# Two graph attention layers from neighbor lists: a reworked prelude, the 20-node block in another PSUM tile, and layer 1 with each product ahead of the next sums

## The chip, the cores and the metric

The kernel runs on one core of one Trainium2 chip. The metric is the device time of one execution in microseconds (us), from the start to the end of the program; the kernel before has a median of 1781.02 us. A core has five engines with instruction queues of their own: PE (TensorE, matrix products into PSUM), DVE (VectorE), ACT (ScalarE), POOL (GpSimd) and SP (SyncE, which here only issues DMAs). ACT and POOL issue DMAs too; all gathers and scatters by index are issued by POOL.

## The reference

Two layers on a graph of N = 2708 nodes with features of D = 1024, in f32. `adj` is a dense 2708 x 2708 matrix of 0 and 1 with about 17 ones in a row.

```python
# layer 0
f = x @ Wf + bf;  g = x @ Wg + bg
e = relu(f @ g.T)
att = softmax(where(adj > 0, e, NEG), axis=1)
x = layernorm(x + att @ (x @ W + bW))
# layer 1
h = x @ W1;  f1 = h @ a1;  f2 = h @ a2
e = leaky_relu(f1 + f2.T, 0.2)
att = softmax(where(adj > 0, e, NEG), axis=1)
x = layernorm(x + relu(att @ h))
```

Each node attends to its neighbors alone, so the kernel never forms an N x N product. With M = Wf Wg^T the score of nodes i and j in layer 0 is x_i M x_j plus terms of the biases. In layer 1, f1 = x (W1 a1) and f2 = x (W1 a2), so the two vectors u1 = W1 a1 and u2 = W1 a2 are enough for the scores. In both layers the neighbors' rows are summed first and multiplied with the weight after that: (att @ x) W.

## The kernel before

**Queues.** `pe`, `dve`, `act`, `pool` and `sp` are wrappers (class `InOrder`, L61) that keep what is issued through them in the order of the program text; the profile shows all of it at L71. What is written with `nc.vector` or `nc.gpsimd` instead may be moved by the scheduler of the framework.

**Prelude (L249 to L511).** For each of 22 blocks of 128 rows of `adj` (the last has 20 rows, the "20-node block") `lists(b)` (L402) loads the block into one of three `adj` tiles through SP, ACT casts it and counts its ones (`Relu` with a sum), POOL multiplies it by `iota`, which falls from 8192 along a row (L409), so that a one becomes a number that tells its column, and DVE takes the eight largest of each of 20 segments (`MAX8`, L412) and from these the 40 largest of the row (L414 to L418), and then the number of neighbors and its class (L420 to L425). Three blocks later `keep_lists` (L427) has ACT turn the result into indices and write them to DRAM (`LD`). Beside that runs the generator `weights()` (L292), one step of it for each block: it loads rows of Wg, Wf and W1 (through ACT's queue), turns them on PE (`turned`, L281: eight 128 x 128 transposes for a tile of 128 rows), and computes M in 16 products (`m_product`), two bias rows (`c_product`), and u1 and u2 (`u_product`). The result of a product leaves PSUM for SBUF on ACT one step later (the list `late`, emptied by `flush`). `row_parts` (L252) splits a bias row into three bf16 rows on POOL: three casts, three small DMA issues and two subtractions. Many constants are filled by POOL at the head of the program (L150 to L233).

When all blocks are done, each node gets its place by the number of its neighbors (L451 to L502, the "rank stage"): the results `ids`, the node at each place, and `idq`, where its list lies. Places are cut into 22 new blocks of 128 (block 0 has 20 nodes in 32 places), and these into 85 groups of 32. A group of class t has `TILES` = t tiles, and a tile is one gather of 128 rows: four neighbors for each of the group's 32 nodes. Block 0 has 3 tiles, blocks 1 and 21 have 15, blocks 19 and 20 have 16, blocks 2 to 18 have 20: 405 gathers in each layer.

**Layer 0 (L757 to L985)** takes the blocks as units in the order 1, 0, 2, ..., 21. A unit's rows x are gathered (`load_x`), turned, and multiplied by M (`f_product`), the result is replicated four times (`Fr`, on ACT); POOL gathers the neighbors' rows into a ring of 20 slots; DVE forms one dot product for each tile (`dots`) and the softmax weights (`soft`); PE sums the weighted rows (`Layer.sums`, L693: first the row sums `rs`, then one half of a tile after the other into the PSUM tile `po`), turns the sum y and multiplies it by W, held in `Wt`; `close` (L828) adds x and norms. The result goes to X1S and, with f2 = x u2 in a further column, is scattered by POOL to the table T1. The PSUM pool `ps_m` has two tiles `pm`, `ps_t` has two tiles `pt`, `ps_s` one tile `po`. L858 to L906 are the start: unit 1's product is made in two halves (L877), then the 20-node block's (`f_small`, L799, with `split_product`, L558, which spreads its 8 steps over four groups of 32 columns and lets a second matmul with `rep` add the four parts), then unit 2's (`f_product(2)`); ACT issues the load of W into `Wt` (4.19 MB) at L900, behind the copies that precede it in the program.

**Layer 1 (L988 to L1111)** takes the blocks in the order 0 to 21 with a ring of 32 slots (`ring` and `more`). The rows of T1 are gathered; DVE forms the scores from the f2 column (`scores1`); in step k PE forms the sums of block k, and then the product of block k-1 with W1 (`M` holds W1 by then), and then turns y of block k (L1079 to L1089). `close1` (L1027) takes relu, the residual and the norm of the block before that, and its scatter to the output is issued inside a later block's sums (the hook 6 at L1079). After the last step come the last turn, the last product (in two PSUM tiles) and the closing of the last two blocks. A slot of the ring is free, and the gather for it is issued, where the sums have used it (L725 to L727).

## Time and profile before

| | us |
|---|---|
| median of 3 runs (1780.73 to 1785.28) | 1781.02 |
| the profiled execution's own time | 1778.93 |
| its span, first to last instruction | 1777.1 |
| of it: prelude and rank stage, 0 to 218 | 218 |
| layer 0, 218 to the first gather of layer 1 | 939 |
| layer 1, 1157 to the end | 620 |

The same three stretches by engine (busy us):

| stretch | PE | DVE | ACT | POOL | DMA engines' mean share |
|---|---|---|---|---|---|
| 0 to 218 | 171.1 | 171.8 | 109.4 | 162.6 | 54% |
| 218 to 1157 | 877.6 | 773.8 | 445.5 | 589.1 | 72% |
| 1157 to 1777 | 524.4 | 225.9 | 81.5 | 430.8 | 90% |

The profile is one execution. "Busy" is the time in which an engine works on an instruction; what an engine waits for is told by the waits (waiter, releaser, total, times, longest) and by the timelines (start, duration, engine, line, operation, output and inputs, and in brackets the idle time before it and what ended it). A row "x8" stands for eight like instructions in a row with their total. In the page's slices, the span is cut in 40 equal parts, here of 44.4 us, and a digit is the busy share in tenths. The load of W by ACT is a DMA: its engine is busy for the issue alone, and the transfer shows in the DMA share.

### The profile page before, as it was taken

How to read it: one execution, taken by the hardware profiler on the slowest of the kernel's cores; microseconds unless marked ns; L12 is line 12 of the kernel's file. 1: busy time of each engine (PE TensorE's matmuls, PEld its weight loads, DVE VectorE, ACT ScalarE, POOL GpSimd, SP SyncE). 2: the span in 40 equal slices, each digit the busy share in tenths (PEclk: the TensorE clock that was granted, in tenths of full speed). 3: DMA queues.
4: the chain of work that ended last, by engine and by line, in shares of the span. 5: the costliest groups of instructions: out<-in, count | busy, mean ns of one | idle time of the engine just before them, and what ended most of it. 6: DMA issues, size and time to landing. Idle time of an engine off the chain costs nothing. (4 is left out here: it accounts for less than half of the span.)

```text
span 1777.1 us, 22911 instructions
## 1 busy us (share of the span) xinstructions
PE 1573.1 (89%) x7313; PEld 667.6 (38%) x7313; DVE 1171.4 (66%) x3539; ACT 636.4 (36%) x861; POOL 1182.5 (67%) x1191
## 2 busy tenths in 40 slices
PE   4999479899999999999999999637989988989996
PEld 2444234344444444444444444213333333333342
DVE  5879855888888888988888887513342433424442
ACT  4544454444444455555555544101111111111111
POOL 7878476467666666666666663177777777777740
PEclk9999779999999999999999999959989999999998
DMA  7646168568777777777777777299999999999960
GB/s 283 237 169 238 40 233 301 208 224 296 282 285 274 264 250 255 280 284 287 279 291 283 268 281 281 103 358 346 363 386 392 392 364 394 384 392 388 366 259 37
DMA packets 149982, 501.86 MB, mean 282 GB/s; under 512 B 32565, under 2 KB 32597, under 8 KB 147144
## 3 DMA queue, kind: packets, MB, share of 16 engines
q0 software_dynamic: 132032, 427.36, 64.8%
q1 hardware_dynamic: 10202, 55.72, 8.3%
q10 hardware_dynamic: 7618, 17.23, 2.7%
q8 instruction: 59, 0.97, 0.2%
q14 instruction: 71, 0.58, 0.1%
HBM read 509.64 MB, written 33.75 MB: 306 GB/s over the span
## 5 line engine op out<-in xcount | busy, mean ns | idle before, releaser
L71 POOL DMA_INDIRECT ring<-in_x_dram,SL x405 | 432.0, 1067 | 256.2 <-issue 89.0
L71 DVE SCALAR_TENSOR_TENSOR j<-ring,Fr 128x1024 bf16<-128x1024 f32 x402 | 494.9, 1231 | 77.0 <-DMA ring<-in_x_dram,SL 49.8
L71 ACT COPY Fr<-pm 32x1024 f32<-32x1024 f32 (+2 forms) x353 | 340.5, 965 | 20.0 <-PE pm L71 15.3
L71 PE MATMUL po<-ring,st 128*32 128x512 f32 x2660 | 338.6, 614 | 0.1
L71 POOL DMA_INDIRECT ring<-T,SL x260 | 259.6, 998 | 83.8 <-issue 58.0
L71 PE MATMUL pm<-M,xT 128*128 128x512 f32 (+1 forms) x704 | 309.7, 617 | 0.4 <-ACT xT L71 0.4
L71 PE MATMUL pm<-Wt,xT 128*128 128x512 f32 (+1 forms) x704 | 303.5, 599 | 0.0
L71 PE MATMUL pm<-M,yT 128*128 128x512 f32 (+1 forms) x704 | 298.5, 595 | 0.3 <-ACT yT L71 0.3
L71 ACT ACTIVATE scores<-scores 128x24 f32<-128x24 f32 (+5 forms) x44 | 9.8, 222 | 640.7 <-DVE scores L71 640.7
L71 PEld LDWEIGHTS pm<-M,yT 128*128 128x128 f32 (+1 forms) x704 | 127.2, 186 | 170.2 <-issue 169.7
L71 PEld LDWEIGHTS pm<-M,xT 128*128 128x128 f32 (+1 forms) x704 | 127.0, 190 | 170.6 <-issue 169.9
L71 PEld LDWEIGHTS pm<-Wt,xT 128*128 128x128 f32 (+1 forms) x704 | 125.0, 186 | 151.8 <-issue 151.4
L71 POOL DMA_INDIRECT more<-T,SL x145 | 144.1, 994 | 44.0 <-issue 32.8
L71 PEld LDWEIGHTS po<-ring,st 128*32 128x32 f32 x2660 | 102.5, 114 | 183.9 <-issue 180.0
L71 DVE TENSOR_SCALAR scores<-ring,f1q 128x2 f32<-128x2 f32 (+5 forms) x98 | 21.8, 245 | 211.3 <-DMA ring<-T,SL 209.6
L409 POOL TENSOR_TENSOR adj<-adj,iota 128x2708 f32<-128x2708 f32 (+3 forms) x23 | 130.5, 5684 | 24.9 <-ACT adj L71 24.8
L71 ACT ACTIVATE y<-po,ri 128x512 f32<-128x512 f32 (+1 forms) x88 | 55.8, 683 | 232.5 <-PE po L71 214.6
L412 DVE MAX8 cand<-adj 128x8 f32<-128x136 f32 (+2 forms) x440 | 97.2, 284 | 37.4 <-POOL adj L409 37.4
L71 PE MATMUL pm<-halfT,WfT 128*128 128x512 f32 x256 | 113.9, 600 | 1.1 <-ACT WfT L71 1.1
L71 POOL DMA_INDIRECT SL<-LD,idq x85 | 85.5, 1006 | 25.8 <-issue 20.9
L71 PE MATMUL pt<-rs,stack 128*32 128x1 f32 x680 | 14.1, 179 | 98.0 <-DVE rs L71 53.4
L71 PE MATMUL po<-more,st 128*32 128x512 f32 x580 | 94.2, 651 | 0.0
(198 smaller groups left out, 1416.9 us busy)
## 6 DMA issues: line engine op xcount, KB each, us to landing
adj<-in_adj_dram SPq DMA_DIRECT2D x21, 1354.0 KB, 5.8
X1S<-z SPq DMA_DIRECT2D x20, 512.0 KB, 6.4
ring<-in_x_dram,SL POOLq DMA_INDIRECT x405, 6.2
u1b<-X1S SPq DMA_DIRECT2D x11, 512.0 KB
rb<-X1S SPq DMA_DIRECT2D x10, 512.0 KB, 7.3
ring<-T,SL POOLq DMA_INDIRECT x260, 7.3
rows<-in_L_gnn_Wg_dram ACTq DMA_DIRECT2D x8, 512.0 KB, 4.5
rows<-in_L_gnn_Wf_dram ACTq DMA_DIRECT2D x8, 512.0 KB, 3.6
```

Of the source, the lines that this page charges most:

```text
L71: made = self.tc.keep_in_program_order(op(*args, **kwargs))
L409: nc.gpsimd.tensor_tensor(k[:n, cut], k[:n, cut], iota[:n, cut], op=ALU.mult)
L412: nc.vector.max(cand[:n, s, :], k[:n, s * SEG:min((s + 1) * SEG, N)])
```

## The change

Three parts of the program change.

*Prelude.* u1 and u2 are no longer made on PE. The eight turned tiles of W1, `u_product` and the loads for them go; `W1` is loaded whole into `Wt` by SP at the start of layer 0, `a1` and `a2` are broadcast to all partitions by two DMAs of POOL in the middle of the prelude (into `u1b` and `u2b`), 16 dot products on DVE (`u_dots`) give the two columns, and `u_spread` brings them back into `u1b` and `u2b` as rows on all partitions: 16 matmuls and four ACT copies. There are four `adj` tiles instead of three. The first block is loaded, cast and multiplied in two parts, the second block is multiplied in two. The 20-node block of `adj` comes in the middle of the order instead of last, as four quarters of its columns on four groups of partitions (`tail`), so that a segment's `MAX8` serves four. The constants are filled by `pool` in four batches after the third to the sixth block. `weights()` yields a cost at each step (1 for a turned tile, 6 for a product), and the loop takes steps up to 6.5 units a block. POOL does one multiply (`same` by `early`) of the rank stage, whose tiles come from a pool of their own, `places`.

*Start of layer 0.* The 20-node block's product uses the sums' tile `po` (`ps_s`) for its first part and no longer waits for one of the two `pm`; unit 2 is turned earlier; `f_product(2)` comes directly after that, and the 20-node block's second part after that. The issue of the load of W now stands behind `u_spread`'s copies.

*Layer 1.* The blocks are ordered by the number of their tiles (0, 1, 21, 19, 20, 2, ..., 18). In step k the sums of a block are followed by the turn and the product of the same block, and by its `close1`; its scatter is issued inside the next block's sums.

The diff, cut to what matters (a removed line of one of the functions printed above is left out in places, and so is the rank stage but for its multiply):

```diff
+        def constants():
+            pool.memset(quad, 0.0)
+            for q in range(Q):
+                rows = slice(32 * q, 32 * q + 32)
+                pool.tensor_copy(stack[rows], ident[rows, rows])
+                pool.memset(quad[rows, q:q + 1], 1.0)
...
+                pool.memset(t, v)
+            yield
...
-        with tc.tile_pool(name="adjp", bufs=3) as adjp, tc.tile_pool(name="cands", bufs=2) as cands, \
+        with tc.tile_pool(name="adjp", bufs=4) as adjp, tc.tile_pool(name="cands", bufs=2) as cands, \
...
-                def u_product(h, wT):
...
                 WgT[1] = half_tile()
                 for k in range(KC):
-                    flush()
                     turned(WfT[:, :, k * P:(k + 1) * P])
+                    yield 1
...
+                        row_parts(brow[:, half], b3[:, half])
+                    yield 6
...
-                flush()
+                    yield 6
                 c_product(1)
-                yield
-                flush()
...
+                yield 6
...
+                if b == NB - 1:
+                    k = tail.bitcast(F32)
+                    act.activation(k, tail, AF.Relu, accum_out=tails)
+                    cand4 = cands.tile([P, NSEG // 4, 8], F32, name="cand4", bufs=1)
+                    for c in range(4):
+                        rows = slice(32 * c, 32 * c + 32)
+                        pool.tensor_tensor(k[rows], k[rows], iota[rows, c * quarter:(c + 1) * quarter],
+                                                op=ALU.mult)
+                    for s in range(NSEG // 4):
+                        nc.vector.max(cand4[:, s, :], k[:, s * SEG:min((s + 1) * SEG, quarter)])
+                    for c in range(4):
+                        rows = slice(32 * c, 32 * c + n)
+                        nc.vector.tensor_copy(cand[:n, c * NSEG // 4:(c + 1) * NSEG // 4, :], cand4[rows])
+                        pool.tensor_copy(tail4[:n, c:c + 1], tails[rows])
...
+                else:
+                    t = adjp.tile([P, N], I32, name="adj")
+                    k = t.bitcast(F32)
+                    cuts = [slice(0, 10 * SEG), slice(10 * SEG, N)]
+                    for i, cut in enumerate(cuts if b == 0 else [slice(0, N)]):
+                        sp.dma_start(t[:n, cut], adj[b * P:b * P + n, cut])
+                    for i, cut in enumerate(cuts if b == 0 else [slice(0, N)]):
+                        act.activation(k[:n, cut], t[:n, cut], AF.Relu,
+                                       accum_out=tot[:n, b:b + 1] if i == 0 else tot2[:n])
+                        if b == 0 and i == 0:
+                            load_weights(3)
+                    for cut in cuts if b < 2 else [slice(0, N)]:
+                        pool.tensor_tensor(k[:n, cut], k[:n, cut], iota[:n, cut], op=ALU.mult)
...
+            blocks = list(range(NB - 1))
+            blocks.insert(NB // 2, NB - 1)
+            steps, done, some = weights(), 0, constants()
+            act.activation(tot2, ones, AF.Relu)
+            for i, b in enumerate(blocks):
                 lists(b)
-                if b > 2:
-                    keep_lists(b - 3)
-                if b == 4:
...
+                if 2 <= i < 6:
+                    next(some, None)
+                if i == 6:
+                    pool.memset(tail, 0)
+                    for c in range(4):
+                        pool.dma_start(tail[32 * c:32 * c + few, :], adj[N - few:, c * quarter:(c + 1) * quarter])
+                if i == 8:
                     fill_highs()
-                if b > 0:
-                    next(steps, None)
-            for b in range(NB - 3, NB):
+                if i in (13, 15):
+                    u, a = (u1b, a1) if i == 13 else (u2b, a2)
+                    pool.dma_start(u, a.rearrange("d o -> (d o)").partition_broadcast(P))
+                flush()
+                while done < (2 * i if i < 3 else 6.5 * i - 13.5):
+                    cost = next(steps, None)
+                    if cost is None:
+                        break
+                    done += cost
+            for b in blocks[-3:]:
                 keep_lists(b)
             for _ in steps:
...
+            nc.gpsimd.tensor_tensor(same, same, early, op=ALU.mult)
...
+    def split_product(xT, w, parts, row=None, pm=None):
...
+        pm = ps_m.tile([P, H, 512], F32, name="pm") if pm is None else pm
...
+        yield
...
+        sp.dma_start(Wt, W1.rearrange("(k p) d -> p k d", p=P))
...
-        def f_small():
-            pm = whole(split_product(xTs.pop(0), M, yp.tile([P, D], F32, name="y"), 0))
...
+        def u_dots(k0, k1):
+            for k in range(k0, k1):
+                for i, u in enumerate((u1b, u2b)):
+                    dot(Wt[:, k, :], u, P, ucols[:, i, k:k + 1])
+        def u_spread(i):
+            u = (u1b, u2b)[i]
+            pts = []
+            for k0 in range(0, KC, 4):
+                pt = ps_t.tile([P, 4, P], F32, name="pt")
+                for k in range(4):
+                    pe.matmul(pt[:, k, :], ucols[:, i, k0 + k:k0 + k + 1].to_broadcast([P, P]), ident,
+                              start=True, stop=True)
+                pts.append(pt)
+            yield
+            for k0, pt in zip(range(0, KC, 4), pts):
+                act.copy(u[:, k0 * P:(k0 + 4) * P], pt.rearrange("p k i -> p (k i)"))
...
         load_lists(0)
+        u_dots(0, 2)
         q_dot(1)
...
+        u_dots(2, KC)
+        for _ in spread0:
+            pass
+        xTs[2] = tp.tile([P, KC, P], F32, name="xT")
+        turn2 = turn(xb[2], nrows[2], xTs[2])
+        next(turn2)
+        small_f = split_product(xTs.pop(0), M, yp.tile([P, D], F32, name="y"), 0,
+                                ps_s.tile([P, H, 512], F32, name="po"))
+        next(small_f)
...
+            for _ in turn2:
+                pass
+        next(small_f)
...
-        f_small()
-        x_turn(2)
...
+        spreads = [u_spread(0), u_spread(1)]
+        next(spreads[0])
         f_product(2)
+        for _ in spreads[0]:
+            pass
+        next(spreads[1])
+        Fr[0, 0] = zs[:, :D]
+        act.copy(Fr[0, 0], flat(whole(small_f)))
+        for _ in spreads[1]:
+            pass
         spread2 = q_spread(2)
         next(spread2)
         act.dma_start(Wt, W.rearrange("(k p) d -> p k d", p=P))
...
-        first_gathers(5, NSL0)
+        for g in range(5, max(g for _, g, _ in lay.order[:lay.count]) + 1, 4):
+            first_gathers(g, g + 4)
...
+        order1 = sorted(range(NB), key=lambda b: (sum(TILES[g] for g in groups[b]), b))
+        units = cut(R1, Q, order1)
...
-        waiting = []
         for k, u in enumerate(units):
...
-                count_over()
-            lay.sums(u, po, {6: [lambda s=closing: [None for _ in s]]}, y[b])
-            closing = iter(())
-            if back is not None:
-                if back > 0:
-                    prod[back] = product(P, yTs.pop(back)[0], M)
-                else:
-                    prod[back] = whole(split_product(yTs.pop(back)[0], M, z1[1]))
+            y = yp.tile([P, D], F32, name="y1")
+            lay.sums(u, po, {6: [lambda s=closing: [None for _ in s]]}, y)
             yT = tp.tile([P, KC, P], F32, name="yT")
-            steps = turn(y.pop(b), nrows[b], yT, halves=True)
-            next(steps)
-            yTs[b] = yT, steps
-            if waiting:
-                closing = close1(waiting.pop())
-                next(closing)
-            if back is not None:
-                waiting.append(back)
-            if nxt is not None:
-                scores1(nxt)
+            for _ in turn(y, nrows[b], yT, halves=True):
+                pass
+            if k + 1 == NB:
+                prod = two_products(P, yT, M)
+            elif b > 0:
+                prod = product(P, yT, M)
+            else:
+                prod = whole(split_product(yT, M, z1[1]))
             for i in (2 * k, 2 * k + 1):
                 if i < NB:
                     mark_over(i)
+            if k == NB // 2 + 1:
+                count_over()
+            if k + 1 < NB:
+                scores1(units[k + 1])
+            closing = close1(b, prod)
+            if k + 1 < NB:
+                next(closing)
             if k + 2 == NB:
                 unfit = nc.values_load(flag[0:1, 0:1])
         for _ in closing:
             pass
-        b = NB - 1
-        for _ in yTs[b][1]:
-            pass
-        prod[b] = two_products(P, yTs.pop(b)[0], M)
-        for b in waiting + [b]:
-            for _ in close1(b):
-                pass
     return unfit
```

## The prediction

> **What bounds the kernel now.** I read the page first (engines, then slices), then the waits of the first 206 us, the engines' timelines at the start of layer 0, and POOL's and PE's timelines at the end of layer 1. The page:
>
> ```profile
> span 1777.1 us, 22911 instructions
> PE 1573.1 (89%) x7313; PEld 667.6 (38%) x7313; DVE 1171.4 (66%) x3539; ACT 636.4 (36%) x861; POOL 1182.5 (67%) x1191
> ...
> PE   4999479899999999999999999637989988989996
> ...
> DMA  7646168568777777777777777299999999999960
> ```
>
> No engine is the limit throughout. Slices 1 to 5 (to 220 us) are the prelude. Slices 6 to 25 are layer 0, where PE stands at 9 and DMA at 7; its loop, which the change leaves alone from the third unit on, is PE's. Slices 26 to 38 are layer 1 with DMA at 9. In the prelude the waits say more than the busy shares:
>
> ```profile
> DVE cand L412 <- POOL adj L409: 37.4, 13, 12.8
> ACT M L71 <- PE pm L71: 33.1, 9, 5.0
> ACT adj L71 <- DMA adj<-in_adj_dram: 25.6, 7, 7.5
> POOL adj L409 <- ACT adj L71: 24.8, 11, 7.2
> ```
>
> (Columns: waiter, releaser, us in total, times, longest.) DVE's sort of 22 adjacency blocks sets the end, and it starves: POOL's product is late because ACT's relu is late, because ACT queues behind copies of matmuls, or because the three `adj` tiles are all held. DVE begins at 13.8, ends the lists at 206.0, and the indices `ids` are complete at 217.9. At layer 1's end POOL's timeline (start, us, what, idle before) reads
>
> ```profile
> 1707.46 0.99 POOL L71 DMA_INDIRECT ring<-T,SL  x1 [0.30 <-issue]
> 1708.75 0.99 POOL L71 DMA_INDIRECT ring<-T,SL  x1 [0.30 <-issue]
> 1710.05 0.99 POOL L71 DMA_INDIRECT more<-T,SL  x1 [0.30 <-issue]
> ```
>
> one gather each 1.295 us without a gap since 1157.4: 404 steps x 1.295 = 523, 18 scatters 24, memsets and hiccups 6, sum 553 = 1710.05 - 1157.4. POOL's issue rate bounds layer 1; the transfers keep pace. Then PE:
>
> ```profile
> 1724.36 1.04 PE L71 MATMUL pt<-ident,y 128*128 128x128 f32 x8
> 1725.69 0.31 PE L71 MATMUL pt<-rs,stack 128*32 128x1 f32 x16 [0.29 <-ACT yT L71]
> ...
> 1732.82 14.00 PE L71 MATMUL pm<-M,yT 128*128 128x512 f32 x32
> 1746.66 1.04 PE L71 MATMUL pt<-ident,y 128*128 128x128 f32 x8
> 1747.99 14.00 PE L71 MATMUL pm<-M,yT 128*128 128x512 f32 x32 [0.29 <-ACT yT L71]
> ```
>
> The last sums (1725.8) are followed by the product of the block before (1732.8) and only then by their own (1748.0): 14 us of the tail belong to an earlier block.
>
> **What the skill says.** Trainium skill, "DMA: Bandwidth & Descriptors", section "Issuing engines are not separate DMA queues": DMAs from ACT, SP and POOL run on the same 16 engines and interleave. The trace agrees: from 276 to 280 us the load of W took 53% of the engines and the gathers 50%. "TensorE: Matmul & The Clock Gate", section "What's actually happening": the clock halves after about 3.4 us of idle. Here an idle of 2.69 us at 1655.5 was followed by about 3 us of matmuls at 1.07 us, one of 2.34 at 1629.1 was not.
>
> **Part 1, the prelude.** Removed from PE: 8 turned W1 tiles at 1.1 us of transposes (8.8) and two `u_product`s at 7.1 (14.2), 23 us. PE then has 16 tiles (18), 16 M products at 7.1 (114) and two c products (14): 146 us, spread at 6.5 units a block, 7.7 us, beside DVE's 7.3 to 8.2. Four `adj` tiles take away the 25.6 us wait: a tile's turn is load 5.8, relu 2.7, POOL 5.9, sort 7.5, sum 22, which three tiles give every 7.3 us and four every 5.5.
>
> What is next late is POOL. The order of the built kernel puts both `row_parts` of bW (6.8 us each: three casts of 0.6, three issues of 0.5, two subtractions of 1.15, gaps) right before the third and fourth block's products, and the constants (about 1 us a batch) before the next ones. POOL, from the halved first block (load of half about 5.0, relu 1.4, product from 6.7): blocks 0, 1 done at 12.7 and 18.9, block 2 at 31.6, block 3 at 45.6, block 4 at 52.8, then 6 to 7 a block, tail at 104, block 13 at 130.3 (a `row_parts` more), block 20 at 173. DVE against this, with 4.1 us for the 20 MAX8 and 4.0 for the chain, 0.22 for each pair member where two blocks are interleaved: from 9.7, blocks 0 and 1 done at 27, block 2 31.6 to 39.9, blocks 3 and 4 45.6 to 62.2, block 7 started at 78.6, block 10 done 109.5, the tail (5 MAX8, 4 copies, chain: 5.9) 115.4, block 14 144, block 17 167, block 20 191.7. The two early stalls (about 5 and 6 us) stay; later DVE is never without work. ACT's lists for block i-3 stand before its copies, so relu(i) comes about 8 us after DVE ends block i-4, 8 us before POOL's result is needed: hidden. End of the lists 191.7 instead of 206.0, **-14.3**. The rank stage loses one DVE multiply (0.64) to POOL: **-0.5**. `c3`'s last parts on POOL end near 201, `ids` at 203, so the first gather isn't held (2 us of cover).
>
> W1's load on SP waits for the last c product, about 167; 4.19 MB in 13 to 14 us (the load of W took 14) is there by 182. Four dots at 1.28 (5.1 us) fit before the first `xb` lands (5.55 us idle at 217.9), twelve (15.3) in the 14.64 us that DVE idles at 230 to 244.9: about 0.5 late, 0. Without that cover they cost 20. The two broadcasts of a1, a2 are one POOL issue each, in the sum above.
>
> **Part 2, the start of layer 0,** on the clock of before (all of it shifts by 14.8). Now:
>
> ```profile
> 263.81 1.04 PE L71 MATMUL pt<-ident,xb 128*128 128x128 f32 x8
> ...
> 280.13 0.31 PE L71 MATMUL pt<-rs,stack 128*32 128x1 f32 x16
> ...
> 293.91 7.13 PE L71 MATMUL pm<-Wt,xT 128*128 128x512 f32 x16
> ```
>
> The small block waited 9.19 us for a `pm` tile (to 254.0). In `po` it runs at 245.8 to 252; the f product takes the freed `pm` at 255.4 (the ACT copies are 1.1 later for xT) and ends at 270.3, then 8 u matmuls (1.1) and the replication (2.0): first sums at 273.6, against 280.1; DVE is ready at 272.9. That is -6.5. But ACT's issue of W now stands behind copies of `u2b`, which stand behind the replication: 275.7 instead of 264.9. In before it was alone for most of its 14 us; now gathers for the third unit start at 276 and take half: 4.19 MB at 205 GB/s is 20.4 us, landing at 298.3. PE wants it at 287.6 (293.9 - 6.3). The product goes to 298.4, and third sums from 327.1 to about 329: **+2**. Bounds: W in time, DVE then sets the third sums at 321.3, -5.8; slow clock after the 11 us idle, +4. I take +2, since the shared rate is measured.
>
> **Part 3, layer 1.** Units ordered by tiles (3, 15, 15, 16, 16, then 17 of 20); each product follows its own turn. PE's round of 20 tiles: row sums 0.4, sums 8.85, wait for y 0.86 and transposes 1.23 (as at 1125), wait 0.29, product 13.86: 25.5. POOL's round: 20 gathers and a scatter, 21 x 1.295 = 27.2. So POOL stays the bound. At the start PE lags by up to 6.5 us on units 2 to 4 (sums at 1214, 1238, 1262), but slot reuse asks for less: POOL reaches tile 81 at 1268, freed at 1263. Scatters fall 6 gathers after the sums start and their block is normed 7.2 us after it, POOL reaches them 13.7 after: hidden. DVE's order (scores, then close, then the next reciprocal) leaves the reciprocal 3 us before it is used.
>
> End: 20 scatters instead of 18 stand before the last gather, +2.6: issued at 1712.7; row sums ready 10.9 later, as before (1710.05 to 1721.0): 1723.6; sums of 20 tiles to 1732.9; turn 2.4; product 14.0, 1749.3; and 15.1 from the last product to the end (1762.0 to 1777.1): 1764.4. **-12.7**. Bounds: -6 (PE late by 6) and -14 (no second scatter).
>
> **Sum.** -14.3 - 0.5 + 2 - 12.7 = -25.5, on a span of 1777.1: 1751.6. That execution took 1778.93, 1.8 around its span, and the runs' median 1781.02 is 2.1 above it. Carrying both: 1755.5.
>
> **Rivals.** (A) The sum above, 1755.5, own range 1747 to 1764: 0.60. (B) The prelude gains little: POOL, whose 160 us of work stay, slips a few us in each of the 22 products, or ACT's lists tie relu to DVE; lists end near 203, gain 3: 1768. For it: DVE already ran at 19.3 of 20 from 140 to 200. Against: 37.4 us of starvation lie ahead of that. 0.18. (C) Everything fits: the row parts wait elsewhere, DVE runs through (9.7 + 21 x 7.5 + 5.5 = 173, but POOL's 173 + 8 forbids less than 181), -25; W in time, -6; tail -14: 1738. 0.14. (D) Slower: PE becomes layer 1's bound. Its gap of 1.15 a unit was seen only in layer 0 and singly; over 17 units at 27.2, a round of 29.0 eats the 25.5 and 5 more. At 29.5 (a gap of 5 us, clock down after it) it is +39: 1794. Against: 1746.66 to 1747.99 shows the turn-to-product wait at 0.29. 0.08. That the dots' move saves nothing is in B: PE was not DVE's only cover.
>
> **Chances.** 0.3% (5.3 us) is what a measurement can tell from no change: faster below 1775.7, B's upper fringe (0.03) lies at it. Faster 0.60 + 0.15 + 0.14 = 0.89; same 0.04; slower 0.07. Range 1740 to 1770: A, nearly all of B, half of C.
>
> **What would show it.** DVE's first MAX8 near 10, lists' end near 192 with idles of about 5 before blocks 2 and 3; no wait of ACT on `adj` loads of several us; the first sums (unit 1) at about 259 and the first Wt product at about 283.5, after an idle of PE near 11; POOL at 1.295 a gather through layer 1; last product directly behind the last turn, and 52 us from the last gather's issue to the end, where it was 67. It is wrong if POOL has gaps in layer 1 (D), or if DVE waits past block 4 (B).

## The result and the profile after

The changed kernel takes 1771.74 us (median of 6 runs, 1765.66 to 1779.03) beside 1781.88 us (6 runs, 1780.73 to 1785.39) for the kernel before: ratio 0.9936, interval 0.9917 to 0.9955. It is faster by 10.1 us. 25.5 were forecast, and 1771.74 lies 1.7 above the range. The profiled execution took 1770.84 us with a span of 1769.1, against 1778.93 and 1777.1: 8.0 us of span to account for. Read by marks in both traces (the end of the last list, taken at the first instruction of the rank stage; the first gather of layer 0; the third unit's sums; the first and the last gather of layer 1; the end):

| stretch | before | after | difference | predicted |
|---|---|---|---|---|
| prelude, to the end of the lists | 206.1 | 202.9 | -3.2 | -14.3 |
| rank stage, to the first gather | 12.7 | 15.1 | +2.4 | -0.5 |
| start of layer 0, to the third sums | 108.2 | 110.8 | +2.6 | +2.0 |
| layer 0's loop | 830.3 | 829.3 | -1.0 | 0 |
| layer 1, first to last gather issued | 552.7 | 561.0 | +8.3 | +2.6 |
| tail, to the end | 67.0 | 49.9 | -17.1 | -15.3 |
| sum | 1777.1 | 1769.1 | -8.0 | -25.5 |

So the end of layer 1 came about as foretold and the prelude did not. The page of the kernel after, engines and slices:

```profile
span 1769.1 us, 22760 instructions
PE 1563.6 (88%) x7217; PEld 660.3 (37%) x7217; DVE 1198.7 (68%) x3559; ACT 629.2 (36%) x840; POOL 1188.8 (67%) x1210
...
PE   4799289899999999999999999839998988889896
...
DMA  7655268567777777777777787289999999999990
```

PE's 23 us of products for u1 and u2 are gone from its first slices, yet the prelude still fills five of them. The waits of its first 206 us (waiter, releaser, us in total, times, longest):

```profile
ACT M L71 <- PE pm L71: 22.8, 8, 5.4
...
DVE cand L423 <- POOL adj L71: 16.1, 6, 8.6
DVE cand L423 <- POOL quad L71: 12.7, 1, 12.7
ACT adj L71 <- DMA adj<-in_adj_dram: 10.3, 10, 2.7
...
POOL adj L71 <- ACT adj L71: 6.7, 4, 2.7
```

ACT's wait for `adj` loads fell from 25.6 to 10.3 and POOL's for ACT from 24.8 to 6.7, as was predicted. But DVE still waits 16.1 + 12.7 = 28.8 us for POOL (37.4 before), and 12.7 of that in one piece, ahead of block 2. POOL's timeline there (start, us, what, idle before and what ended it):

```profile
23.74 0.60 POOL L265 CAST part<-u1b 1x512 bf16<-1x512 f32 x1 [4.98 <-DMA u1b<-in_L_gnn_bW_dram]
...
31.52 0.60 POOL L265 CAST part<-rest 1x512 bf16<-1x512 f32 x1 [2.27 <-DMA rows<-part]
32.41 0.53 POOL L266 DMA_DIRECT2D rows<-part  x1 [0.29 <-POOL part L265]
32.96 5.93 POOL L71 TENSOR_TENSOR adj<-adj,iota 128x2708 f32<-128x2708 f32 x1
38.81 0.12 POOL L71 MEMSET quad<- 128x4 f32 x1
```

The row parts of bW stand ahead of block 2's product, as predicted; that POOL would wait 4.98 us for bW itself and 2.27 us for a row's DMA was not predicted. Block 2 is ready at 38.9 instead of 31.6.

The start of layer 0:

```profile
265.10 0.38 PE L71 MATMUL pm<-rows,ones 3*128 3x512 bf16 x1
265.42 7.13 PE L71 MATMUL pm<-M,xT 128*128 128x512 f32 x16
...
279.79 9.63 PE L71 MATMUL po<-ring,st 128*32 128x512 f32 x60 [0.22 <-issue]
...
295.68 4.56 PE L71 MATMUL pm<-Wt,xT 128*128 128x512 f32 x10
```

The 9.19 us wait for a `pm` tile is gone, but the first sums stand 61.1 us after the first gather, where they stood 61.3, and they take 9.63 us. In the kernel before they took 7.07:

```profile
280.58 7.07 PE L71 MATMUL po<-ring,st 128*32 128x512 f32 x60
```

The product with `Wt` begins without a wait for the load of W. And the end of layer 1, POOL and PE:

```profile
1717.87 0.99 POOL L71 DMA_INDIRECT ring<-T,SL  x1 [0.30 <-issue]
1719.17 0.99 POOL L71 DMA_INDIRECT more<-T,SL  x1 [0.30 <-DMA out_dram<-z,ids]
```

```profile
1713.69 14.00 PE L71 MATMUL pm<-M,yT 128*128 128x512 f32 x32
1728.84 0.29 PE L71 MATMUL pt<-rs,stack 128*32 128x1 f32 x14 [1.15 <-DVE rs L71]
...
1738.61 1.24 PE L71 MATMUL pt<-ident,y 128*128 128x128 f32 x8 [0.85 <-ACT y L71]
1739.99 14.00 PE L71 MATMUL pm<-M,yT 128*128 128x512 f32 x32
```

The last product follows its own turn directly; the 14 us of an earlier block's product between the last sums and it are gone. POOL still issues one gather each 1.295 us.

### The profile page after: what moved, and what is told of

Read it like the earlier page. It is cut to its first block, busy times and chain, and to the rows that moved or that the text cites. A ratio compares the mean times of both kernels' runs of the same rounds, so it can differ in the third digit from the quotient of the medians.

```text
span 1769.1 us, 22760 instructions
## 1 busy us (share of the span) xinstructions
PE 1563.6 (88%) x7217; PEld 660.3 (37%) x7217; DVE 1198.7 (68%) x3559; ACT 629.2 (36%) x840; POOL 1188.8 (67%) x1210
## 5 line engine op out<-in xcount | busy, mean ns | idle before, releaser
L71 ACT COPY Fr<-pm 32x1024 f32<-32x1024 f32 (+2 forms) x353 | 340.7, 965 | 20.9 <-PE pm L71 16.2
L71 PE MATMUL pm<-M,xT 128*128 128x512 f32 x672 | 306.5, 610 | 0.0
L71 PEld LDWEIGHTS pm<-M,xT 128*128 128x128 f32 x672 | 126.8, 194 | 162.7 <-issue 162.7
L71 DVE TENSOR_SCALAR scores<-ring,f1q 128x4 f32<-128x4 f32 (+4 forms) x98 | 21.3, 233 | 206.7 <-DMA ring<-T,SL 202.6
L71 POOL TENSOR_TENSOR adj<-adj,iota 128x2708 f32<-128x2708 f32 (+2 forms) x23 | 124.6, 5432 | 10.2 <-ACT adj L71 6.7
L423 DVE MAX8 cand<-adj 128x8 f32<-128x136 f32 (+1 forms) x420 | 93.2, 284 | 28.7 <-POOL adj L71 16.1
L71 POOL DMA_INDIRECT SL<-LD,idq x85 | 86.7, 1021 | 25.8 <-issue 20.9
L71 ACT ACTIVATE z<-z,sh,rstd 128x1024 f32<-128x1024 f32 (+1 forms) x32 | 39.7, 1241 | 142.9 <-DVE sh L71 141.2
L71 DVE TENSOR_SCALAR scores<-more,f1q 128x3 f32<-128x3 f32 (+3 forms) x64 | 15.1, 244 | 108.9 <-DMA more<-T,SL 108.9
```

The costliest lines, as they stand in the source:

```text
L71: made = self.tc.keep_in_program_order(op(*args, **kwargs))
L423: nc.vector.max(cand[:n, s, :], k[:n, s * SEG:min((s + 1) * SEG, N)])
```

## The experiments

The theory was that DVE's lists end the prelude and that what delays them delays everything. The rivals: that POOL or ACT slip instead and tie DVE down (rival B), and that the start or layer 1 swallow the gain. "Changed kernel" is the kernel after; an edit is against it unless another is named. Stretches and marks come from each run's own trace. A kernel's time differs from execution to execution (1765.66 to 1779.03 us for the changed kernel), and its two profiled executions differ most in layer 0's loop (829.3 and 838.5), whose code is the same in all kernels and which takes 829 to 844 us in all but the last runs below, on another chip. So the ratios judge a kernel and the marks judge a mechanism.

**The 20-node block's four copies.** DVE collects the 20-node block's results with four copies of 20 x 40 elements (L402). In the timeline of the kernel after:

```profile
112.80 11.83 POOL L71 TENSOR_TENSOR adj<-adj,iota 128x2708 f32<-128x2708 f32 x2 [3.12 <-DVE L L427]
...
114.92 1.11 DVE L399 MAX8 cand<-tail 128x8 f32<-128x136 f32 x5
116.06 9.11 DVE L402 COPY cand<-cand 20x40 f32<-20x40 f32 x4
```

They take 9.11 us while POOL multiplies. The second of them is the longest. It begins 0.1 us after a multiply, and the two end together:

```profile
118.71 5.92 POOL L71 TENSOR_TENSOR adj<-adj,iota 128x2708 f32<-128x2708 f32 x1
118.81 5.85 DVE L402 COPY cand<-cand 20x40 f32<-20x40 f32 x1
```

The edit writes them as an operation that also accumulates:

```diff
-  nc.vector.tensor_copy(cand[:n, c * NSEG // 4:(c + 1) * NSEG // 4, :], cand4[rows])
+  nc.vector.tensor_scalar(cand.rearrange("p s e -> p (s e)")[:n, c * 40:c * 40 + 40],
+                          cand4.rearrange("p s e -> p (s e)")[rows], 0.0, 0.0,
+                          op0=ALU.add, op1=ALU.add, accum_out=tail4s[:n, c:c + 1])
```

> The changed kernel, in which the four pieces of the 20-node block's candidates (20x40) are moved by a tensor_scalar that also writes a sum, instead of a plain copy. Theory (the plain copy waits while POOL's multiplies hold what both engines share): the four take about 4 x 0.26 = 1.1 us instead of 9.1, all that follows is 8 us earlier, the lists end near 195 instead of 202.8, the time is near 1764. Rival 1 (moving 20 rows to other partitions is itself slow): the four still take about 9 us, 1772. Rival 2 (POOL bounds the prelude anyway): the four are short, but DVE then waits for POOL's products of blocks 11 to 20 and the lists end above 200, 1769 to 1772.

Measured 1771.25 us, ratio 0.9941 (0.9926 to 0.9957). All instructions of that line, the shortest, median and longest in ns:

```profile
L403 DVE TENSOR_SCALAR_CACHE_REDUCE cand<-cand x4: 181/182/185, 115.1 to 115.7; 20x40 f32<-20x40 f32 x4
```

With the 0.07 us read of each accumulator it is about 1 us instead of 9.11, while POOL multiplies just as before (112.01 to 123.86). The lists end at 198.1 instead of 202.9: 4.8 of 8 us come through, since DVE then waits longer for POOL's products (21.8 instead of 18.6 from 20 us on). So the cause of the 9.11 us is shown, and the rival of a slow move to other partitions is out. In the total the gain can't be seen: 1771.25 beside 1771.74 and, in a second measurement of the changed kernel, 1771.72.

**POOL's row parts in the order of the text,** so that they can't be moved ahead of block 2's product:

```diff
-  nc.gpsimd.tensor_copy(t, rest)
-  nc.gpsimd.dma_start(dst[i:i + 1], t)
+  pool.tensor_copy(t, rest)
+  pool.dma_start(dst[i:i + 1], t)
...
-  nc.gpsimd.tensor_tensor(same, same, early, op=ALU.mult)
+  pool.tensor_tensor(same, same, early, op=ALU.mult)
```

> The changed kernel with the row parts of the bias rows, and the multiply of same by early, in POOL's program order: the two row parts of bW stand behind the products of the sixth and the tenth block instead of in front of those of the third and fourth, and the last row part of c3 stands in front of the multiply of the rank stage. Theory: DVE's stall of 12.7 us before block 2 shrinks to about 4, that of 5.3 before block 3 goes; POOL has 13.6 us to fit in later, of which 3 to 6 show as stalls; lists end at 195 to 198 instead of 202.8; the rank stage is 2.5 us shorter because POOL no longer works beside DVE there. Time 1762 to 1766. Rival (POOL's sum of work sets the end of the lists): the stalls come back before blocks 6 to 10, the lists end at 201 to 203, only the rank stage gains: 1769 to 1772.

Measured 1773.86, ratio 0.9954 (0.9939 to 0.9970). DVE's wait ahead of block 2 falls from 12.7 to 3.9, but its other waits for POOL's products rise from 5.9 to 11.7 (20 to 206 us), and the lists end at 200.9. In the rank stage DVE now waits 5.0 for `same`, which stands behind the last row parts: 18.2 instead of 15.1. In this order the time of the parts shows at later blocks and in the rank stage instead.

**Three `adj` tiles.** The changed kernel with one number back:

```diff
-  with tc.tile_pool(name="adjp", bufs=4) as adjp, ...
+  with tc.tile_pool(name="adjp", bufs=3) as adjp, ...
```

> The changed kernel with three adj tiles instead of four. The prediction: a tile's turn of 22 us is given every 7.3 us by three tiles and every 5.5 by four, so with three DVE waits now and then: lists end 5 to 12 us later than 202, time 1778. Rival (POOL's order, not the tiles, is what starves DVE): lists end within 2 us of 202, 1771.

Measured 1768.22, ratio 0.9925 (0.9906 to 0.9945). The lists end at 196.0, 6.9 us earlier than with four. The waits of its first 206 us:

```profile
ACT adj L71 <- DMA adj<-in_adj_dram: 44.2, 14, 8.5
...
DVE cand L423 <- POOL adj L71: 23.7, 10, 8.4
...
DVE cand L423 <- POOL quad L71: 6.1, 1, 6.1
```

ACT's wait for the loads rises from 10.3 to 44.2, and the lists don't end later for it. With three tiles a fourth load of 1.4 MB isn't ahead of bW's 4 KB, whose first cast starts at 18.77 instead of 23.74, and the wait ahead of block 2 halves. The tail's copies, all of its instances:

```profile
L402 DVE COPY cand<-cand x4: 172/173/176, 109.5 to 110.1; 20x40 f32<-20x40 f32 x4
```

0.7 us in all, as no POOL multiply runs at 109.5. So the 9.11 us above are no property of the copy. It is these copies, and not the tile, that make the lists end 6.9 us earlier: DVE's waits for POOL are even 1.0 longer than with four tiles (19.6 and 18.6 from 20 us on). Beside the kernel with the copies replaced, whose lists end at 198.1, three tiles are 2.1 us earlier. The fourth tile's effect is this small, and not to its credit.

The prelude's books close with these (DVE's waits for POOL from 20 us to the end of the lists, plus the tail's copies; the first 20 us are alike):

| kernel | waits | copies | sum | lists end |
|---|---|---|---|---|
| after | 18.6 | 9.1 | 27.7 | 202.9 |
| copies replaced | 21.8 | 1.0 | 22.8 | 198.1 |
| three tiles | 19.6 | 0.7 | 20.3 | 196.0 |
| the start mended, second form (below) | 14.0 | 1.0 | 15.0 | 191.0 |

**The exponential ahead of the copies.** ACT's copy of the 20-node block's product waits for PE, and the first unit's exponential stands behind it:

```diff
-  next(spreads[1])
-  Fr[0, 0] = zs[:, :D]
-  act.copy(Fr[0, 0], flat(whole(small_f)))
-  for _ in spreads[1]:
-      pass
   spread2 = q_spread(2)
   next(spread2)
+  small_pm = whole(small_f)
   act.dma_start(Wt, W.rearrange("(k p) d -> p k d", p=P))
...
   soft(units[0])
+  Fr[0, 0] = zs[:, :D]
+  act.copy(Fr[0, 0], flat(small_pm))
...
+  for _ in spreads[1]:
+      pass
```

> The changed kernel, in which ACT's copies of the 20-node block's product and of the second of the two vectors u stand behind the exponential of unit 1's scores instead of in front of it. Theory (at the start of layer 0 the exponential waits 7 us on ACT behind a copy that waits for PE): first sums 2.5 to 4 us earlier and at full clock, third sums 2.5 to 4 us earlier, time 1768. Rival (DVE's dots set the third sums anyway): the first sums come earlier, the third stay within 0.5 us, 1771.

Measured 1771.02, ratio 0.9936 (0.9913 to 0.9960). The start takes 105.0 us instead of 110.8 (108.3 in the changed kernel measured a second time), and the first sums come 58.0 after the first gather instead of 61.1. They are also as short again as in the kernel before:

```profile
275.07 7.07 PE L71 MATMUL po<-ring,st 128*32 128x512 f32 x60 [0.25 <-DMA SL<-LD,idq]
```

In the total this lies within the loop's scatter.

**The same kernel once more,** and **the last parts issued before the last lists:**

> The changed kernel itself once more, on the chip of the three runs beside it, as their base. Its first measurement: 0.9936 of before, a sum of stages: lists end 202.8, indices 217.1, third sums 328.8, first gather of layer 1 at 1158.2, span 1769.1. Expected again: 0.993 to 0.995; stages up to the third sums within 2 us of these; the length from the third sums to layer 1's first gather between 829 and 839, as the six profiled executions so far have it.

Measured 1771.72, ratio 0.9956 (0.9940 to 0.9973): the result stands.

```diff
-  for b in blocks[-3:]:
-      keep_lists(b)
   for _ in steps:
       pass
   flush()
+  for b in blocks[-3:]:
+      keep_lists(b)
```

> The changed kernel, in which ACT takes the last c product out of PSUM before, and not after, it writes the last three blocks' lists, so that POOL makes the last row parts while DVE still sorts. Theory (the rank stage is 2.4 us longer than before because DVE and POOL work at the same time): rank stage 14.2 us becomes about 11.5, indices near 214; time 1769. Rival (nothing at the start of layer 0 is carried to the end): indices earlier, time unchanged.

Measured 1772.02, ratio 0.9954 (0.9939 to 0.9969). The rank stage stays at 15.1. This missed its aim: ACT's copy came early, but the parts on POOL stood behind `same` all the same (`same` at 202.94, parts from 204.14 to past 211), so they still ran beside DVE's comparisons.

**A start that is only later.** Ten further copies of the comparisons for `hot` in the rank stage, which leave the results as they are:

```diff
-  for b0, b1 in ((0, NB // 2), (NB // 2, NB)):
+  for b0, b1 in ((0, NB // 2), (NB // 2, NB)) * 6:
```

> The changed kernel with ten more copies of DVE's two comparisons of the rank stage (their results are the same), which delays the indices by 11 to 13 us. If the start is carried to the end: 1784, ratio 1.000. If layer 0's loop absorbs a shift of its start: below 1777, ratio under 0.997.

Measured 1783.61, ratio 1.0028 (1.0012 to 1.0045). The rank stage grows by 10.7, the time by 11.9 over the 1771.72 of the changed kernel's second measurement. So nothing behind the prelude absorbs such a delay; what the prelude failed to give is missing at the end.

**The start mended.** The copies, the order of POOL's program, the last parts before the last lists, and the exponential together, with all row parts after POOL's last product:

```diff
-  act.dma_start(brow, bW.rearrange("(o d) -> o d", o=1))
+  act.dma_start(u2b[0:1, :], bW.rearrange("(o d) -> o d", o=1))
...
-  row_parts(brow[:, half], b3[:, half])
...
+  for h in range(2):
+      row_parts(u2b[0:1, h * 512:(h + 1) * 512], b3[:, h * 512:(h + 1) * 512])
+  pool.dma_start(u2b, a2.rearrange("d o -> (d o)").partition_broadcast(P))
+  for b in blocks[-3:]:
+      keep_lists(b)
```

> The changed kernel with the start mended in four places: the 20-node block's pieces moved in the form with a sum, all three late row parts behind POOL's last product, the last c product taken out before the last lists, and the exponential of unit 1 in front of the copies. Theory (POOL's order and the copies cost the prelude what the prediction missed): lists end at 182 to 187 instead of 202.8, indices at 194 to 199, third sums near 303, 25 us earlier; carried to the end, 1747, ratio 0.980. Rival (layer 0's loop takes back what its start gains, as two runs suggest): same stages, but 1760 to 1770.

Measured 1761.57, ratio 0.9880 (0.9857 to 0.9904). The lists end at 185.5, but the rank stage takes 22.7, for this line of its timeline:

```profile
198.58 0.66 DVE L498 TENSOR_REDUCE rank<-same 128x22 f32<-128x484 f32 x1 [8.28 <-POOL same L71]
```

`same` on POOL waits behind 20 us of row parts. Hence a second form, in which DVE keeps this multiply and one row part comes in the middle of the prelude:

```diff
+  if i == 15:
+      row_parts(u2b[0:1, :512], b3[:, :512])
...
-  for h in range(2):
-      row_parts(u2b[0:1, h * 512:(h + 1) * 512], b3[:, h * 512:(h + 1) * 512])
+  row_parts(u2b[0:1, 512:], b3[:, 512:])
...
-  pool.tensor_tensor(same, same, early, op=ALU.mult)
+  nc.vector.tensor_mul(same, same, early)
```

> As the run with the start mended, but the multiply of same by early is on DVE again (0.64 us), and one of bW's two row parts lies in the middle of the prelude, where POOL runs ahead. Theory (in that run DVE waited 8.3 us for POOL's multiply, which stood behind 20 us of row parts): lists end at 184 to 187, rank stage 12.5 to 14 instead of 22.7, indices at 197 to 200, third sums at 303 to 306, 23 us before the changed kernel; time 1749, ratio 0.982. Rival (a start that comes earlier meets something else late, such as W1's load or the dots): indices as said, third sums not before 310, 1757 to 1762.

Measured **1752.43, ratio 0.9831 (0.9814 to 0.9849)**, the lowest median of all. Its waits of DVE from 20 to 212 us:

```profile
DVE cand L422 <- POOL adj L71: 10.3, 4, 5.0
DVE cand L422 <- POOL quad L71: 3.7, 1, 3.7
```

Lists at 191.0 and the first gather at 203.8, a rank stage of 12.8: what was predicted for the kernel after (191.7, and `ids` at 203). The third sums come 20.9 and 17.6 us earlier than in the changed kernel's two traces, and the time is 19.3 us less, so this gain is carried to the end.

**The third part alone, and its order.** The kernel before with layer 1 of the kernel after:

```diff
+  order1 = sorted(range(NB), key=lambda b: (sum(TILES[g] for g in groups[b]), b))
+  units = cut(R1, Q, order1)
...
+  for _ in turn(y, nrows[b], yT, halves=True):
+      pass
+  if k + 1 == NB:
+      prod = two_products(P, yT, M)
```

> The kernel before with the third part of the change alone: layer 1 ordered by tiles, each product after its own turn. The prediction: 12.7 us less than before (1769). By the trace of the changed kernel, whose layer 1 is 8.8 us shorter in one execution: 1773, with 20 scatters in front of the last gather instead of 17 (+4) and the tail from the last gather's issue to the end near 50 us instead of 67. Rival (layer 1 gains nothing beyond noise, since POOL's issue sets its length): ratio above 0.997.

Measured 1774.61, ratio 0.9963 (0.9947 to 0.9978): -6.6 us by the ratio, -9.4 by its trace (layer 1 from 619.7 to 610.3). Then the same with the blocks in their natural order, here and in the mended kernel:

```diff
-  order1 = sorted(range(NB), key=lambda b: (sum(TILES[g] for g in groups[b]), b))
+  order1 = list(range(NB))
```

> The kernel before with each product of layer 1 directly after its own turn, but the blocks in the old order. Theory: the tail shrinks from 67 to 47.5, three more scatters stand before the last gather (+4), POOL's hiccups +3: 12 us less, 1769; the sorted order alone (ratio 0.9963) gave away 2 of them. Rival (sorted order is needed): ratio above 0.9963.

> As the run with same on DVE, and layer 1 in the order 0 to 21 instead of sorted by tiles. Theory: POOL sets layer 1's pace in any order, and the last block has 15 tiles instead of 20, so its sums are 2.2 us shorter: tail 47.5 instead of 49.7, time 2 us less, 1747. Rival (the sorted order is what lets PE keep pace at the start): POOL has gaps before the third and fourth block, 1752.

Measured 1775.63, ratio 0.9960 (0.9943 to 0.9977), and 1755.09, ratio 0.9851 (0.9825 to 0.9877). No difference to the order by size in either pair. The marks show two effects that cancel: from the first to the last gather 554.6 and 555.9 instead of 560.6 and 558.4, and the tail 55.8 and 57.4 instead of 49.7 and 50.3. PE's end in the mended kernel with the natural order:

```profile
1702.62 14.00 PE L71 MATMUL pm<-M,yT 128*128 128x512 f32 x32 [0.15 <-ACT yT L71]
1716.55 0.31 PE L71 MATMUL pt<-rs,stack 128*32 128x1 f32 x16
```

The blocks of 15 and 16 tiles come last, POOL gathers them in fewer us than PE's 14-us product and sums take, and PE runs behind without a gap: the shorter tail that was expected there did not come.

**On another chip.** Three more kernels were measured, twice each, on a chip on which the kernel before itself takes 2001.55 and 2007.17 us: the mended kernel with both row parts at the end; that with three `adj` tiles; the changed kernel with layer 1 of before. The edit of the first, against the second mended form:

```diff
-  if i == 15:
-      row_parts(u2b[0:1, :512], b3[:, :512])
...
-  row_parts(u2b[0:1, 512:], b3[:, 512:])
+  for h in range(2):
+      row_parts(u2b[0:1, h * 512:(h + 1) * 512], b3[:, h * 512:(h + 1) * 512])
```

> As the run with same on DVE, with both row parts of bW behind POOL's last product. In that run DVE still waited 5 us for the block behind the row part in the middle. Theory: lists end at 184 to 186 instead of 191.0; the rank stage 13 to 15 us because POOL works beside it; third sums near 303; time 1747 to 1750, ratio 0.980 to 0.982. Rival (the row parts now make the indices late): rank stage over 17 us, 1752 to 1755.

> The same with three adj tiles. If the fourth tile matters once POOL's order is right, as the prediction says of a tile's turn of 22 us: lists end 5 us later or more, at 190 or above, 1753. If the loads of the fourth tile only take bandwidth from the weights at the start: lists end at 184 or earlier, 1747.

> The changed kernel with layer 1 as it was before: its prelude and start of layer 0 alone. The prediction gave these 12.8 us (1768, ratio 0.993). By the traces of the changed kernel (third sums at 325.5 and 328.8 against 327.1): nothing beyond 2 us, ratio 0.998 to 1.001.

> All row parts behind POOL's last product, same on DVE, exponential first, pieces in the form with a sum; on another chip. Lists end at 184 to 186, rank stage 15 to 17 us (16.8 in the run on the slow chip), third sums 304 to 306, about as in the run with one part in the middle: time 1750 to 1753, ratio 0.982 to 0.984. If the rank stage takes 13: 1747.

> The same with three adj tiles, on another chip. The prediction's view of the fourth tile (a turn of 22 us): lists end 5 us later or more. Other view (its loads only take bandwidth from the weights at the start): lists end within 2 us of the run with four, time equal.

> The changed kernel with layer 1 as it was before: its prelude and start of layer 0 alone, on another chip. The prediction gave these 12.8 us (1768, ratio 0.993). By the traces of the changed kernel (third sums at 325.5 and 328.8 against 327.1): nothing beyond 2 us, ratio 0.998 to 1.001.

Measured: 1.0930 (1.0850 to 1.1009) and 1.0872 (1.0776 to 1.0968) for the first two, 1.0900 and 1.0968 again; 0.9988 (0.9939 to 1.0037) for the third, and 2005.89 beside 2007.17 again, medians of runs that differ by up to 80 us. By the traces layer 1 takes 957.9 and 959.9 us in the first kernel and 764.4 and 767.1 in the third. So on this chip the new layer 1 costs some 193 us, a tenth of the time. ACT's waits in layer 1 of the first:

```profile
ACT y L71 <- remote: 363.7, 21, 22.8
```

and PE's in a part of it (1300 to 1700 us):

```profile
PE pt L71 <- ACT y L71: 136.7, 8, 21.2
```

ACT's read of y from PSUM waits 17 us on average, 21 times in 22 blocks, for a cause that the trace calls "remote" (it could not be traced to an instruction of this core) and does not explain. With the old layer 1, in the third kernel, this wait is even longer:

```profile
ACT y L71 <- remote: 521.1, 19, 31.5
```

But there PE has the product of the block before to do in that time, and in the same 400 us none of its waits is for y. In the changed order sums, y, turn, product and the next sums form one chain and PE stands still (in the kernel after, on its chip, PE's wait for y in the same 400 us is 13.1, longest 0.9). These totals say nothing on the prelude edits. The preludes, which show no such wait, do: with four tiles the lists end at 186.2 and 185.1 and the first gather goes out at 203.0 and 201.8; with three at 185.3, 184.1 and 200.3, 199.1. The fourth tile buys nothing here either. Both row parts at the end lengthen the rank stage to between 15.0 and 16.8, 2 to 4 us over the 12.8 of the second mended form, so the first gather comes 0.8 to 4.7 us earlier than the 203.8 there. Whether that gives a shorter time on an ordinary chip was not measured.

## Why the prediction was wrong

**The prelude's sum (-14.3, measured -3.2) is the step that failed,** in two terms. First the 20-node block: "5 MAX8, 4 copies, chain: 5.9" priced the copies at nearly nothing, as they are when POOL is idle (0.7 us in all). They took 9.11 because POOL's 5.93 us multiplies ran. The Trainium skill, "SBUF — State Buffer", section "Who interferes with whom", says that a copy on DVE can enter a mode that needs the pair of ports shared with POOL, and that who comes second is blocked for the other's whole instruction, while a form that also writes out its accumulator is exempt. The traces agree on each point: a longest copy of 5.85 us that ends with the multiply begun 0.1 us before it, and 0.18 us in the accumulating form beside the same multiplies. The prediction did not ask what ran on POOL at the moment of the copies. Second, "block 2 at 31.6, block 3 at 45.6" counted POOL's instructions and not what they wait for: bW's 4 KB, queued behind loads of `adj` and of weights, and a row's DMA. Both blocks came 7 us later. The stall ahead of block 3 was itself as predicted (5.3 us), the one ahead of block 2 was not (12.7 instead of 5), and after that DVE never waited more than 0.3 us for a product. Together the terms overshoot the miss (8 + 7 against 11), because they overlap: with the copies replaced DVE waits 3.2 us longer for POOL.

**"Four `adj` tiles take away the 25.6 us wait" was read wrongly.** The wait went, and nothing was won: with three tiles it was 44.2, and the lists end 2.1 us earlier than with four, where the copies cost next to nothing in both (196.0 and 198.1). It was slack of an engine that isn't the limit, and the fourth load delayed a 4 KB one that was on the path. Other steps hold: the first MAX8 came at 9.6 (near 10 predicted), and with the two terms repaired the lists do end at 191.0. That this is so near 191.7 is partly luck: the row parts were moved there, and the stalls lie elsewhere (3.7 us ahead of block 2, 5.0 behind the part in the middle).

**The rank stage (-0.5, measured +2.4).** The multiply that moved to POOL saves DVE 0.65, but the prediction asked only whether POOL's last row parts hold the first gather, not what runs beside them. DVE's timeline of the kernel after:

```profile
203.84 1.42 DVE L488 TENSOR_TENSOR gt<-cls,classes 128x242 f32<-128x242 f32 x1
...
207.78 0.62 DVE L504 TENSOR_SCALAR hl<-ranki 128x22 int32<-128x22 int32 x1
...
209.54 2.09 DVE L516 TENSOR_TENSOR hot<-hlf,highs 128x935 bf16<-128x935 f32 x1
...
211.55 1.29 DVE L512 TENSOR_TENSOR low<-low,rows 128x704 bf16<-128x704 f32 x1
```

The same four in the kernel before:

```profile
206.44 0.39 DVE L455 TENSOR_TENSOR gt<-cls,classes 128x242 f32<-128x242 f32 x1
...
210.38 0.18 DVE L474 TENSOR_SCALAR hl<-ranki 128x22 int32<-128x22 int32 x1
...
211.70 1.13 DVE L486 TENSOR_TENSOR hot<-hlf,highs 128x935 bf16<-128x935 f32 x1
212.74 0.88 DVE L482 TENSOR_TENSOR low<-low,rows 128x704 bf16<-128x704 f32 x1
```

That is 2.84 us lost. POOL at the moment of the first two, in the kernel after:

```profile
203.73 1.25 POOL L484 TENSOR_TENSOR same<-same,early 128x484 f32<-128x484 f32 x1 [19.64 <-DVE same L483]
...
207.77 0.60 POOL L265 CAST part<-rest 1x512 bf16<-1x512 f32 x1
```

So the first of the four ran beside the very multiply that had moved, and lost 1.03 us to save 0.65; the others ran beside casts and a subtraction of the row parts. The same section of the skill says that a DVE instruction with two inputs in SBUF contends with a POOL instruction that reads SBUF. Three of the four have two inputs, and for them the traces agree. The second has one input and took 0.62 us, as long as the cast that began 0.01 us before it; this sentence does not cover it. With POOL out of the way and the multiply back on DVE the stage is 12.8 us (second mended form).

**The start of layer 0 (+2, measured +2.6): the right size for a wrong reason, which is luck.** W was in time: ACT issued its load at 276.2, and PE began the product at 295.7 without waiting. But the 6.5 us at the first sums did not come either. ACT had put the first unit's exponential behind the copy of the 20-node block's product, which waited for PE, and DVE behind that (timeline of the kernel after):

```profile
276.09 1.01 ACT L71 COPY z<-pm 128x1024 f32<-128x1024 f32 x1 [13.34 <-PE pm L71]
...
278.23 0.73 DVE L71 TENSOR_TENSOR st<-scores,stack 128x384 f32<-128x384 f32 x2 [7.01 <-ACT scores L71]
```

"DVE is ready at 272.9" on the clock of before named the engine, but not what its last step waits for on ACT. The exponential put first gave 3 to 6 us back. The +2.6 itself arose inside the first sums: they stood as far from the first gather as before, but took 9.63 us instead of 7.07, and PE's granted clock (its share of full speed) was 0.77 from 279 to 292 us. In the kernel before it was 1.00 in its first sums (280 to 290), and with the exponential first 1.00 again (274 to 285). A slow clock stood among the prediction's bounds (+4), but the sum left it out.

**Layer 1 (-12.7, measured -8.8, and -9.4 alone): right mechanism, one term off.** The tail was foretold as 52 us and is 49.9. From the first to the last gather it lost 8.3 us instead of 2.6. Twenty scatters stand before the last gather instead of 17 (the prediction took 18): 3 x 1.32 = 4.0. POOL's gaps over the usual 0.30 make 4.1 us instead of 1.0, in pauses of 0.7 to 2.0 us at 1270, 1410, 1552 and 1690: 3.1. The rest, 1.2, is spread. PE did not become the bound (rival D): PE's longest wait for y in the middle of layer 1 is 0.9, and POOL's gaps, which were to be D's sign, are far smaller than D's.

**The outcome lies closest to rival B** (1768): the prelude gave 3 us because POOL came late, though for other reasons than its 22 products' pace or ACT's lists, and without the sign that the prediction gave for B, waits of DVE past block 4. That B's number came true is luck in that measure. The chance of 0.60 for the sum, with only 0.18 for B, rested on durations taken without what runs beside them. (Rival C's three terms give 1736 from 1781, not 1738; nothing rests on it.)

## What to carry to other kernels

A duration from a trace holds only for what ran beside it: before a small DVE copy or a two-input operation is priced, look at what POOL does at that moment, and try an accumulating form where they must overlap. A wait in the table is worth removing only if its release is the last thing the next engine waits for; a deeper buffer that removes other waits can delay a small transfer that matters more. When a cross-engine chain is straightened to shorten a tail, the slack that it had in the middle is gone, and a late step of one engine then shows in full.

## What the runs showed beyond that

- In layer 1 with blocks in order of size, POOL pauses 0.7 to 2.0 us about every 140 us (five blocks of 20 tiles); in the natural order, with the same products ahead, such pauses are absent (one gap of 0.59, or two of up to 0.66). The cause is open.
- Layer 0's loop varies from 829 to 844 us between executions with the same code on ordinary chips; on the slower one it takes 873 to 891.
- The 4 KB of bW, queued among loads of `adj` and of weights, could be used at 23.7 us with one more 1.4 MB load ahead of it, and at 18.8 at the latest without.
- One chip ran the kernel before at 2001.55 us. There is no trace of it from there; with the same layer 1 behind the new prelude ACT waited for y up to 31.5 us at a time. Why is not known.
